# A graph sum by sorted scatter: all edges go through the scatter, against a kernel in which 48 columns of edges bypass it

## The chip, the cores and the metric

The kernel runs on one core of a Trainium2 chip. The metric is the device time of one execution in microseconds (us); the number given for a kernel is the median of its runs. The engines are named as in the profile: PE (TensorE, matmuls) with its weight loads PEld, DVE (VectorE), ACT (ScalarE), POOL (GpSimd, which issues the scatter), and SP (SyncE, which here only issues transfers).

## The reference

There are 6250 nodes with 128 features, and 206250 edges, each with a source node and 128 attributes, in no useful order of the source. Only the source is used:

```python
edge_aggr = jnp.zeros((n, HIDDEN)).at[row].add(edge_features)      # row = src: a sum of edge rows by node
combined = jnp.concatenate([x, edge_aggr, global_expand], axis=-1) @ W_c + b_c
h = softplus(combined @ W1 + b1)
h = softplus(h @ W2 + b2)
out = layernorm(x + h @ W3 + b3)
```

The sum over 206250 edges is the work; the small network behind it has 6250 rows.

## The kernel before, in words

**Columns and blocks.** Edge number p*1611 + c lies on partition p in column c, so the edges make 1612 columns of 128 (the last has 42). The nodes make 25 blocks of 256.

**Scatter and sum.** The columns are dealt to ten groups (`GROUPS`). For each group the kernel computes where every edge must go so that the edges of one block become neighbours in HBM, each block's stretch rounded up to whole units of 128, 256 or 512 rows (`positions`: DVE compares, scans and reductions, PE counts with matmuls of ones). `load_rows` brings a piece of ten columns of edge rows into SBUF (tile `rows`, SP queue), `code_rows` writes a number beside each row that names the node in its block and the group (line 597, on ACT), and `scatter_rows` sends the piece to HBM, one indirect transfer of 128 rows per column (line 605, POOL). One group later `reduce_steps` reads the sorted rows back: `load` brings 1024 rows (eight tiles of 128) into a tile `chunks` (SP queue); `match` makes a 0/1 matrix `hot` from the numbers, 256 wide per row (line 404, DVE, all eight tiles in one instruction); `total` multiplies the rows with it on PE (line 419) into the PSUM tile `part`, of which there are two, and DVE adds the result to the block's 256 columns of `sums_t` (line 424). A place in HBM is first filled with -1 (`fill_rows`), so that unused rows match nothing.

**The 48 columns.** The first 48 columns (`DIRECT`) are never scattered. `direct_steps` multiplies each column's 128 rows with a 0/1 matrix over all 6400 nodes, 512 at a time, so that every column meets 13 windows. ACT makes the matrix as relu(1 - |number - node|): one `Abs` per column and window (line 538) and one `Relu` per pair of columns (line 540), with three buffers `direct_hot`; PE multiplies two steps later (line 550) and DVE adds after twelve columns (line 554).

**Order.** PE, DVE, ACT and SP run a written order; all transfers of SP stand in one queue in the order of the program. For every piece of a group the program puts down: the load of the piece three ahead (`LEAD`), the code of the piece two ahead, the scatter of the piece, and then a share of the waiting steps: the positions of the next group, the sums of the group before, filling, and in groups 1 to 6 the 48 columns. The shares are set by `AHEAD`, so that a list is finished after 75% to 95% of the group's pieces. Each engine works through its own part of this order and never past an instruction that waits. After the last group its own sums are left, and then the network.

Of the kernel before, what the change touches and what calls it, by code (L numbers as in the profile page):

```python
# [7 lines left out]
F32 = mybir.dt.float32  # L8
# [35 lines left out]
def kernel(  # L44
# [33 lines left out]

    ND = min(DIRECT, T) // QUAD * QUAD
    c0 = ND  # L80
# [15 lines left out]

    iota_f = const.tile([P, WIDE], F32, name="iota_f")
    nc.gpsimd.iota(iota_f, pattern=[[1, WIDE]], base=0, channel_multiplier=0,
# [65 lines left out]
    with ExitStack() as phase:  # L164
        keep = phase.enter_context(tc.tile_pool(name="keep", bufs=1))
        per = phase.enter_context(tc.tile_pool(name="per", bufs=2))
        hots_p = phase.enter_context(tc.tile_pool(name="in_block", bufs=4))
        rows_p = phase.enter_context(tc.tile_pool(name="rows", bufs=LEAD + 2))
        chunks_p = phase.enter_context(tc.tile_pool(name="chunks", bufs=4))
        direct_p = phase.enter_context(tc.tile_pool(name="direct", bufs=1))  # L170
        hots = phase.enter_context(tc.tile_pool(name="hots", bufs=2))
# [3 lines left out]
        nc.vector.tensor_copy(iota_ps, iota_f[:, :BL])  # L175
# [7 lines left out]
        def whole_nodes(c0, c1):  # L183
# [10 lines left out]
            return part, node, wrap  # L194

        def node_codes(c0, c1):


            n = c1 - c0
            part, node, wrap = whole_nodes(c0, c1)  # L200
# [33 lines left out]
        def positions(g):  # L234
# [86 lines left out]
            def place(k, j0, j1):  # L321
                m = j1 - j0
                pr = by_col(ps.tile([P, 512], F32, name="pr", bufs=2))[:, :, :m]
# [45 lines left out]
            for k, (a, b) in enumerate(parts):  # L369
                for j0 in range(0, b - a, POS_COLS):  # L370
                    j1 = min(b - a, j0 + POS_COLS)
                    if j1 == b - a and k + 1 < len(parts):
                        steps.append(lambda k=k: scan(k + 1))
                    steps.append(lambda k=k, j0=j0, j1=j1: place(k, j0, j1))
                    todo.append(lambda k=k, j0=j0, j1=j1: place2(k, j0, j1))
                    if len(todo) > 1:
                        steps.append(todo.pop(0))
# [4 lines left out]
        def reduce_steps(g):  # L382
# [16 lines left out]
            def match(i):  # L399
# [3 lines left out]
                hot_of[i] = hot  # L403
                nc.vector.scalar_tensor_tensor(  # L404
# [25 lines left out]
            for i in range(n + 1):  # L430
                def one(i=i):
# [4 lines left out]
                    if i:  # L436
                        total(i - 1)
# [68 lines left out]
        def direct_steps():  # L506


            steps = []
            if not ND:  # L510
                return steps
            NW = -(-NB * BL // WIDE)
            less = keep.tile([P, NW, ND], F32, name="less")
            rows_in, hot_of, sum_of = {}, {}, {}

            def begin():

                first = keep.tile([P, NW], F32, name="first")
                nc.gpsimd.iota(first, pattern=[[WIDE, NW]], base=0, channel_multiplier=0,
                               allow_small_or_imprecise_dtypes=True)  # L520
                part, node, _ = whole_nodes(0, ND)
                nc.vector.tensor_copy(node, part)
                nc.vector.tensor_tensor(
                    less, node.unsqueeze(1).to_broadcast([P, NW, ND]),
                    first.unsqueeze(2).to_broadcast([P, NW, ND]), op=ALU.subtract)

            def load(c):
                n = min(SET, ND - c)
                rows_in[c] = direct_p.tile([P, SET, D], F32, name="direct_rows", bufs=2)
                sync_dma(rows_in[c][:, :n],  # L530
                         edge_attr[:P * T, :].rearrange("(p t) d -> p t d", p=P)[:, c:c + n, :])

            def compare(c, w, q):
                n = min(WIDE, NB * BL - w * WIDE)
                hot = direct_p.tile([P, QUAD, WIDE], F32, name="direct_hot", bufs=3)
                hot_of[c, w, q] = hot
                for j in range(QUAD):
                    nc.scalar.activation(hot[:, j, :n], iota_f[:, :n], AF.Abs,  # L538
                                         bias=less[:, w, c + q + j:c + q + j + 1], scale=-1.0)
                nc.scalar.activation(hot[:, :, :n], hot[:, :, :n], AF.Relu, bias=ones[:, :1],  # L540
                                     scale=-1.0)

            def add(c, w, q):
                n = min(WIDE, NB * BL - w * WIDE)
                k = min(SET, ND - c)
                hot = hot_of.pop((c, w, q))
                if q == 0:
                    sum_of[c, w] = ps.tile([P, WIDE], F32, name="direct_sum", bufs=1)
                for j in range(QUAD):
                    nc.tensor.matmul(sum_of[c, w][:, :n], rows_in[c][:, q + j, :], hot[:, j, :n],  # L550
                                     start=(q + j == 0), stop=(q + j == k - 1))
                if q + QUAD == k:
                    here = sums_t[:, w * WIDE:w * WIDE + n]
                    nc.vector.tensor_add(here, here, sum_of.pop((c, w))[:, :n])  # L554

            jobs = [(c, w, q) for c in range(0, ND, SET) for w in range(NW)
                    for q in range(0, min(SET, ND - c), QUAD)]
            steps += [begin, lambda: load(0)]
            for i in range(len(jobs) + 2):
                def one(i=i):  # L560
                    if i < len(jobs):
                        c, w, q = jobs[i]
                        if (w, q) == (NW // 2, 0) and c + SET < ND:
                            load(c + SET)
                        compare(*jobs[i])
                    if i > 1:
                        add(*jobs[i - 2])
                steps.append(one)
            return steps

# [42 lines left out]
        with tc.manual_schedule(engines={ET.PE, ET.DVE, ET.Activation, ET.SP}):  # L613
# [5 lines left out]
            put_dma(nc.scalar, src_i[:, ND:c1], by_part[:, ND:c1])  # L619
            put["todo"] = fill_rows(0)  # L620
            sync_dma(src_i[:, c1:T], by_part[:, c1:])
            if ND:
                sync_dma(src_i[:, :ND], by_part[:, :ND])
# [10 lines left out]
            node_codes(ND, c1)  # L634
# [11 lines left out]
            direct = direct_steps()  # L646


            left = [0.0] * G
            for g in range(1, G - 3):  # L650
                left[g] = max(0.0, groups[g][1] - groups[g][0]
                              - groups[g - 1][3] * groups[g - 1][2] / 3 - (26 if g == 3 else 0))
            direct_at = 0.0
            i = 0
            for g in range(G):
# [8 lines left out]
                for q in mine:  # L664
# [4 lines left out]

                    now = []  # L670
                    for w, todo in enumerate((prep, sums, other, filled)):
                        share = min(1.0, (q - mine[0] + 1) / (AHEAD[w] * len(mine)))
# [156 lines left out]
```

## Time and profile before

| what | value |
| --- | --- |
| time, median of 3 runs (lowest to highest) | 2886.88 us (2881.78 to 2890.8) |
| the profiled execution: its time, its span | 2886.88 us, 2884.8 us |
| first and last scatter start (line 605) | 25.7 us, 2674.6 us |
| scatters, busy, mean of one | 1564, 1497.8 us, 958 ns |
| last matmul of the sums starts (line 419) | 2779.7 us |
| busy: PE, DVE, ACT, POOL | 1931.5, 1376.6, 822.2, 1557.6 us |
| granted PE clock, mean | 0.836 |

The span runs from the first to the last instruction of one execution; the time holds 2.1 us more. A line of groups gives an operation's count, its busy time and the mean of one, and after the bar the time that its engine stood idle just before it, with what ended most of that. The releaser "issue" means that no wait shows in the profile, "remote" that a wait ended on a semaphore whose setter the profile does not tell. A row of windows gives, for a stretch of the span, the length, then busy time and count for each engine, the granted PE clock, the busy share of the DMA engines and GB/s.

### The profile page before, as it was taken

How to read it: one execution, taken by the hardware profiler on the slowest of the kernel's cores; microseconds unless marked ns; L12 is line 12 of the kernel's file. 1: busy time of each engine (PE TensorE's matmuls, PEld its weight loads, DVE VectorE, ACT ScalarE, POOL GpSimd, SP SyncE). 2: the span in 40 equal slices, each digit the busy share in tenths (PEclk: the TensorE clock that was granted, in tenths of full speed). 3: DMA queues.
4: the chain of work that ended last, by engine and by line, in shares of the span. 5: the costliest groups of instructions: out<-in, count | busy, mean ns of one | idle time of the engine just before them, and what ended most of it. 6: DMA issues, size and time to landing. Idle time of an engine off the chain costs nothing. (4 is left out here: it accounts for less than half of the span.)

```text
span 2884.8 us, 22170 instructions
## 1 busy us (share of the span) xinstructions
PE 1931.5 (67%) x6415; PEld 1254.3 (43%) x6415; DVE 1376.6 (48%) x1940; ACT 822.2 (29%) x1185; POOL 1557.6 (54%) x1635
## 2 busy tenths in 40 slices
PE   2267586677678748776667878567871677475874
PEld 0034244334445525454444645245551556354642
DVE  5255255334456316554234544244551665464965
ACT  0255454352233224243332334323320000000034
POOL 5746555566455565555665555655556356444025
PEclk9879698887889868898888888788996888687987
DMA  9688376554566535455534545344553456354421
GB/s 298 203 244 227 121 199 184 147 153 140 155 185 188 157 97 159 145 155 147 159 92 134 160 135 160 99 133 143 159 154 96 127 168 190 113 153 124 120 71 45
DMA packets 415375, 435.49 MB, mean 151 GB/s; under 512 B 37743, under 2 KB 305766, under 8 KB 415254
## 3 DMA queue, kind: packets, MB, share of 16 engines
q1 hardware_dynamic: 365062, 330.71, 40.7%
q0 software_dynamic: 50048, 103.35, 10.9%
q8 instruction: 51, 0.84, 0.1%
q14 instruction: 70, 0.57, 0.1%
q10 hardware_dynamic: 144, 0.02, 0.0%
HBM read 260.90 MB, written 173.03 MB: 150 GB/s over the span
## 5 line engine op out<-in xcount | busy, mean ns | idle before, releaser
L605 POOL DMA_INDIRECT place<-rows,pos x1564 | 1497.8, 958 | 1170.6 <-ACT rows L597 522.3
L419 PE MATMUL part<-hot,chunks 128*128 128x256 f32 x4472 | 1160.0, 415 | 446.1 <-DVE hot L404 274.2
L419 PEld LDWEIGHTS part<-hot,chunks 128*128 128x128 f32 x4472 | 916.0, 209 | 720.6 <-DVE hot L404 307.3
L424 DVE TENSOR_TENSOR sums_t<-sums_t,part 128x256 f32 x781 | 327.9, 420 | 1130.3 <-remote 676.2
L550 PE MATMUL direct_sum<-direct_hot,direct_rows 128*128 128x512 f32 (+1 forms) x1248 | 628.7, 637 | 267.4 <-DVE sums_t L554 137.5
L538 ACT ACTIVATE direct_hot<-iota_f,less 128x512 f32<-128x512 f32 (+1 forms) x624 | 405.0, 696 | 1351.6 <-remote 726.4
L404 DVE SCALAR_TENSOR_TENSOR hot<-chunks,iota_ps 128x2048 f32<-128x2048 f32 (+1 forms) x281 | 636.7, 2268 | 0.0
L550 PEld LDWEIGHTS direct_sum<-direct_hot,direct_rows 128*128 128x128 f32 x1248 | 251.8, 208 | 512.5 <-issue 397.7
L540 ACT ACTIVATE direct_hot<-direct_hot,ones 128x1024 f32<-128x1024 f32 (+1 forms) x312 | 348.1, 1116 | 10.1
L597 ACT COPY rows<-low 128x10 f32<-128x10 f32 (+1 forms) x159 | 30.4, 195 | 475.6 <-DMA place<-rows,pos 393.3
L554 DVE TENSOR_TENSOR sums_t<-sums_t,direct_sum 128x512 f32<-128x512 f32 (+1 forms) x52 | 34.6, 666 | 170.0 <-remote 85.7
L340 DVE TENSOR_REDUCE pos<-at 128x20 int32<-128x500 f32 (+2 forms) x80 | 87.1, 1089 | 2.7
L307 DVE TENSOR_TENSOR_SCAN so_far<-iota_ps,ib 128x1500 bf16<-128x1500 f32 (+5 forms) x29 | 85.7, 2954 | 0.0
L787 POOL TENSOR_TENSOR x_sb<-x_sb,b_all 128x512 f32<-128x512 f32 (+1 forms) x13 | 15.2, 1209 | 106.9 <-DMA x_sb<-in_x 106.9
L338 DVE TENSOR_TENSOR at<-pr,ib 128x500 f32<-128x500 f32 (+2 forms) x80 | 52.8, 660 | 21.2 <-remote 10.0
L716 ACT ACTIVATE away<-z_ps 128x512 f32<-128x512 f32 (+1 forms) x13 | 7.3, 561 | 191.4 <-DMA x_sb<-in_x 180.9
L775 POOL TENSOR_SCALAR y<-y,mv,rs 128x128 f32<-128x128 f32 (+1 forms) x49 | 38.1, 792 | 41.7 <-DVE rs L771 37.7
L324 PE MATMUL pr<-ib,upto_h 128*128 128x500 bf16 (+2 forms) x80 | 33.4, 418 | 39.1 <-DVE at L338 31.9
L325 PE MATMUL pr<-so_far,ones_h 128*128 128x500 bf16 (+2 forms) x80 | 33.5, 419 | 25.0 <-DVE last L310 23.1
L264 PE MATMUL small<-ib,ones_h 128*128 128x500 bf16 (+2 forms) x80 | 25.2, 427 | 29.4 <-DVE ib L253 29.4
L253 DVE TENSOR_TENSOR ib<-block,iota_ps 128x1500 bf16<-128x1500 bf16 (+5 forms) x29 | 44.3, 1551 | 0.0
L326 PE MATMUL pr<-more,ones_h 128*128 128x500 bf16 (+2 forms) x80 | 33.6, 419 | 3.5 <-issue 3.5
(115 smaller groups left out, 434.8 us busy)
## 6 DMA issues: line engine op xcount, KB each, us to landing
chunks<-place SPq DMA_DIRECT2D x278, 516.0 KB
rows<-in_edge_attr SPq DMA_DIRECT2D x155, 640.0 KB
place<-fill SPq DMA_DIRECT2D x252, 258.0 KB
place<-rows,pos POOLq DMA_INDIRECT x1564
x_sb<-in_x SPq DMA_DIRECT2D x24, 256.0 KB
direct_rows<-in_edge_attr SPq DMA_DIRECT2D x4, 768.0 KB
out<-y SPq DMA_DIRECT2D x12, 256.0 KB
chunks<-place SPq DMA_DIRECT2D x3, 258.0 KB
```

The costliest lines, as they stand in the source:

```text
L253: nc.vector.tensor_tensor(ib, block[:, a:b].unsqueeze(1).to_broadcast([P, NB, n]), iota_ps[:, :NB].unsqueeze(2).to_broadcast([P, NB, n]), ...
L307: nc.vector.tensor_tensor_scan(t, iota_ps[:, 1:2].to_broadcast([P, NB * n]), in_block[k][0], 0.0, op0=ALU.mult, op1=ALU.add)
L338: nc.vector.tensor_mul(at, got.pop((k, j0)), in_block[k][1][:, :, j0:j1])
L340: nc.vector.tensor_reduce(pos[:, a - c0 + j0:a - c0 + j1], at.rearrange("p b g -> p g b"), axis=mybir.AxisListType.X, op=ALU.add)
L404: nc.vector.scalar_tensor_tensor(hot[:, :m], chunks[i][:, :m, D:W].to_broadcast([P, m, BL]), float(1 + BL * g), iota_ps.unsqueeze(1).to_br ...
L419: nc.tensor.matmul(part[:, s - q, :], t[:, s * sub + j, :D], hot[:, s * sub + j], start=(j == 0), stop=(j == sub - 1))
L424: nc.vector.tensor_add(here, here, part[:, s - q, :])
L538: nc.scalar.activation(hot[:, j, :n], iota_f[:, :n], AF.Abs, bias=less[:, w, c + q + j:c + q + j + 1], scale=-1.0)
L540: nc.scalar.activation(hot[:, :, :n], hot[:, :, :n], AF.Relu, bias=ones[:, :1], scale=-1.0)
L550: nc.tensor.matmul(sum_of[c, w][:, :n], rows_in[c][:, q + j, :], hot[:, j, :n], start=(q + j == 0), stop=(q + j == k - 1))
L605: s = nc.gpsimd.indirect_dma_start(out=dst, out_offset=bass.IndirectOffsetOnAxis(ap=at, axis=0), in_=rows[:r, j, :], in_offset=None)
L775: nc.gpsimd.tensor_scalar(y[:r, q, :], y[:r, q, :], mv[:r, at + q, 0:1], rs[:r, 1, at + q:at + q + 1], op0=ALU.subtract, op1=ALU.mult)
```

## The change

All 1612 columns are scattered; `direct_steps`, its tiles and its PSUM bank are gone, and the node numbers are made in `node_codes` alone. Pieces have 20 columns, loaded two ahead (before: ten columns, three ahead). The groups are cut anew, with smaller ones at the end. The sums run two steps behind the comparison instead of one, with five `chunks` (four) and three `hot` (two). In the three last groups, `match` gives three of four loads to ACT (eight `Abs` of 256 and one `Relu` of 2048 per load). All step lists finish after 75% of a group's pieces. Three small tables `codes` are made on POOL at the start. `pr`, the PSUM tile of the positions, gets a third buffer; a filling transfer covers 768 rows instead of 512.

```diff
-LOAD_COLS = 10
+LOAD_COLS = 20
-GROUPS = ((40, 1), (120, 2), (200, 4), (240, 4), (240, 4), (240, 4), (212, 4), (140, 2), (88, 2),
-          (44, 1))
+GROUPS = ((40, 1), (120, 2), (210, 4), (240, 4), (240, 4), (240, 4), (200, 4), (126, 2), (84, 2), (56, 1),
+          (34, 1), (22, 1))
-DIRECT = 48
-SET = 12
-WIDE = 512
-QUAD = 2
-FILL = 4
+TAIL = 3
+FILL = 6
-AHEAD = (0.75, 0.95, 0.9, 0.75)
-LEAD = 3
+AHEAD = 0.75
+LEAD = 2
...
-        hots_p = phase.enter_context(tc.tile_pool(name="in_block", bufs=4))
+        hots_p = phase.enter_context(tc.tile_pool(name="in_block", bufs=5))
...
-        chunks_p = phase.enter_context(tc.tile_pool(name="chunks", bufs=4))
-        direct_p = phase.enter_context(tc.tile_pool(name="direct", bufs=1))
-        hots = phase.enter_context(tc.tile_pool(name="hots", bufs=2))
+        chunks_p = phase.enter_context(tc.tile_pool(name="chunks", bufs=5))
+        hots = phase.enter_context(tc.tile_pool(name="hots", bufs=3))
...
+        codes_of = {}
+        for g in range(max(0, G - TAIL), G):
+            codes_of[g] = keep.tile([P, BL], F32, name=f"codes{g}")
+            nc.gpsimd.iota(codes_of[g], pattern=[[1, BL]], base=1 + BL * g, channel_multiplier=0,
+                           allow_small_or_imprecise_dtypes=True)
...
+                if g in codes_of and i % 4 != 3:
+                    for j in range(m):
+                        nc.scalar.activation(hot[:, j], codes_of[g], AF.Abs,
+                                             bias=chunks[i][:, j, D:W], scale=-1.0)
+                    nc.scalar.activation(hot[:, :m], hot[:, :m], AF.Relu, bias=ones[:, :1],
+                                         scale=-1.0)
+                    return
...
-            for i in range(n + 1):
+            for i in range(n + 2):
                 def one(i=i):
                     if i + 2 < n:
                         load(i + 2)
                     if i < n:
                         match(i)
-                    if i:
-                        total(i - 1)
+                    if i > 1:
+                        total(i - 2)
...
-        def direct_steps():
...
-                    if left[g]:
-                        k = int(direct_at + 0.5)
-                        direct_at += len(direct) * left[g] / sum(left) / len(mine)
-                        now.append(direct[k:int(direct_at + 0.5)])
```

More of the change, by code (lines that the diff above doesn't have):

```diff
@@ L77 @@
     groups = []
-    ND = min(DIRECT, T) // QUAD * QUAD
-    c0 = ND
+    c0 = 0
     for size, sub in GROUPS:
@@ L94 @@
     dram = ctx.enter_context(tc.tile_pool(name="dram", bufs=1, space=bass.MemoryType.DRAM))
-    iota_f = const.tile([P, WIDE], F32, name="iota_f")
-    nc.gpsimd.iota(iota_f, pattern=[[1, WIDE]], base=0, channel_multiplier=0,
+    iota_f = const.tile([P, BL], F32, name="iota_f")
+    nc.gpsimd.iota(iota_f, pattern=[[1, BL]], base=0, channel_multiplier=0,
                    allow_small_or_imprecise_dtypes=True)
@@ L166 @@
         per = phase.enter_context(tc.tile_pool(name="per", bufs=2))
-        hots_p = phase.enter_context(tc.tile_pool(name="in_block", bufs=4))
+        hots_p = phase.enter_context(tc.tile_pool(name="in_block", bufs=5))
         rows_p = phase.enter_context(tc.tile_pool(name="rows", bufs=LEAD + 2))
-        chunks_p = phase.enter_context(tc.tile_pool(name="chunks", bufs=4))
-        direct_p = phase.enter_context(tc.tile_pool(name="direct", bufs=1))
-        hots = phase.enter_context(tc.tile_pool(name="hots", bufs=2))
+        chunks_p = phase.enter_context(tc.tile_pool(name="chunks", bufs=5))
+        hots = phase.enter_context(tc.tile_pool(name="hots", bufs=3))
         ps = phase.enter_context(tc.tile_pool(name="ps", bufs=1, space=PSUM))
         iota_ps = ps.tile([P, BL], F32, name="iota_ps")
-        nc.vector.tensor_copy(iota_ps, iota_f[:, :BL])
+        nc.vector.tensor_copy(iota_ps, iota_f)
         src_i = keep.tile([P, TC], I32, name="src_i")
@@ L181, with node_codes @@
         fill = keep.tile([P, FILL * W], F32, name="fill")
-        def whole_nodes(c0, c1):
+        codes_of = {}
[3 more added lines that the diff above has]
+                           allow_small_or_imprecise_dtypes=True)
+        def node_codes(c0, c1):
             n = c1 - c0
@@ L193, in whole_nodes @@
             nc.vector.tensor_add(part, node, wrap)
[L194 to L200, printed above, removed]
             part_i = wrap.bitcast(I32)
@@ L322, in place @@
                 m = j1 - j0
-                pr = by_col(ps.tile([P, 512], F32, name="pr", bufs=2))[:, :, :m]
+                pr = by_col(ps.tile([P, 512], F32, name="pr", bufs=3))[:, :, :m]
                 nc.tensor.matmul(pr, upto_h, in_block[k][1][:, :, j0:j1], start=True, stop=False)
@@ L375, in positions @@
                     todo.append(lambda k=k, j0=j0, j1=j1: place2(k, j0, j1))
-                    if len(todo) > 1:
+                    if len(todo) > 2:
                         steps.append(todo.pop(0))
@@ L504, in node_rows @@
             return steps
-        def direct_steps():
[L509 to L569, printed above, removed]
@@ L618 @@
             by_part = src[:P * T].rearrange("(p t) -> p t", p=P)
-            put_dma(nc.scalar, src_i[:, ND:c1], by_part[:, ND:c1])
+            put_dma(nc.scalar, src_i[:, :c1], by_part[:, :c1])
             put["todo"] = fill_rows(0)
             sync_dma(src_i[:, c1:T], by_part[:, c1:])
-            if ND:
-                sync_dma(src_i[:, :ND], by_part[:, :ND])
             if R:
@@ L633 @@
                 put["todo"].pop(0)()
-            node_codes(ND, c1)
+            node_codes(0, c1)
             for i in range(LEAD - 1):
@@ L644 @@
             sync_dma(b3_row, b3.rearrange("(o d) -> o d", o=1))
[L646 to L653, printed above, removed]
             i = 0
@@ L668 @@
                     i += 1
+                    share = min(1.0, (q - mine[0] + 1) / (AHEAD * len(mine)))
                     now = []
                     for w, todo in enumerate((prep, sums, other, filled)):
-                        share = min(1.0, (q - mine[0] + 1) / (AHEAD[w] * len(mine)))
                         upto = int(round(len(todo) * share))
```

## The prediction

> **What bounds the kernel now.** I read the groups first, because no engine is busy for the whole span.
>
> ```profile
> L605 POOL DMA_INDIRECT place<-rows,pos x1564 | 1497.8, 958 | 1170.6 <-ACT rows L597 522.3
> L419 PE MATMUL part<-hot,chunks 128*128 128x256 f32 x4472 | 1160.0, 415 | 446.1 <-DVE hot L404 274.2
> ...
> L550 PE MATMUL direct_sum<-direct_hot,direct_rows 128*128 128x512 f32 (+1 forms) x1248 | 628.7, 637 | 267.4 <-DVE sums_t L554 137.5
> ```
>
> The scatters follow each other from 25.7 to 2675.5 us, so POOL's busy time and idle time together set nine tenths of the span. Behind the scatter lie 104.6 us of sums and 104.7 us of network. Next come the waits (total us, times, longest), to split POOL's idle time.
>
> ```profile
> ACT direct_hot L538 <- remote: 726.4, 63, 24.8
> DVE sums_t L424 <- remote: 676.2, 70, 33.4
> POOL place L605 <- ACT rows L597: 522.3, 69, 17.0
> POOL place L605 <- issue: 454.3, 1462, 2.6
> ...
> POOL place L605 <- DMA rows<-in_edge_attr: 101.8, 7, 32.9
> ```
>
> "Issue" is the step from scatter to scatter, 454.3 / 1462 = 0.31 us each; with the 0.958 us of one a column costs 1.268 us. The 1564 cost 1983.2 of 2649.8 us, and 666.6 us are true waits. Most end on the code copy at line 597, which stands on ACT's queue behind the comparisons of the 48 columns (lines 538, 540), and these wait for PE to free a buffer. So far it looks as if ACT were the brake. The third view, windows around 2175 us (PE, PEld, DVE, ACT, POOL, clock, DMA), and the timeline show something else.
>
> ```profile
> 2175.00:2205.00 30.00, 0.82 (x4) 0.38 (x2) 0.00 (x0) 0.62 (x3) 22.68 (x25) 0.59 0.17 56
> 2205.00:2232.00 27.00, 0.00 (x0) 0.00 (x0) 0.84 (x2) 0.42 (x2) 15.19 (x16) 0.50 0.19 61
> ```
>
> ```profile
> 2169.62 3.62 PE L419 MATMUL part<-hot,chunks 128*128 128x256 f32 x16
> ...
> 2205.75 0.36 SPq L141 DMA_DIRECT2D chunks<-place  x1
> 2205.76 0.87 DVE L424 TENSOR_TENSOR sums_t<-sums_t,part 128x256 f32 x2 [35.74 <-issue]
> ```
>
> PE has finished the product at 2173.24 us, yet DVE, which waits for it, and SP, which waits for a free buffer, go on 32.5 us later, at the same moment. In between only POOL works, with one scatter after another from 2161.9 to 2224.8 us. The 63 and 70 "remote" waits are of this kind: what PE reports is heard late during a long row of scatters, and POOL and the sums take turns. Whether that is a law of the chip no row says, but the price can be read where ACT compares nothing, in the last stage (windows of line 605, then of line 419; count in brackets).
>
> ```profile
> 2257.60:2675.50 417.90, 212.45 (x222) 0.81 0.51 147
> 2355.00:2421.10 66.10, 38.27 (x40) 0.90 0.62 185
> 2587.00:2675.50 88.50, 42.06 (x44) 0.77 0.44 127
> ```
>
> ```profile
> 2257.60:2675.50 417.90, 260.49 (x998) 207.34 (x997) 0.81 0.51 147
> 2355.00:2421.10 66.10, 55.71 (x224) 45.56 (x223) 0.90 0.62 185
> 2587.00:2675.50 88.50, 52.55 (x195) 40.83 (x194) 0.77 0.44 127
> 2675.50:2780.10 104.60, 86.33 (x339) 63.84 (x337) 0.95 0.35 94
> ```
>
> A load of eight tiles is 16 matmuls. From 2257.6 to 2675.5 us POOL waited 417.9 - 222 x 1.268 = 136.4 us while 62.4 loads were summed: 2.19 us per load. The best stretch gives (66.1 - 50.7) / 14 = 1.10, the last (88.5 - 55.8) / 12.2 = 2.68. This is the stage most like the changed kernel: scatter and sums alone.
>
> **The change part by part.** *Scatters.* 48 more on POOL: 48 x 1.268 = +60.9 us, all on the path. 1612 x 1.268 = 2044.0 us.
>
> *The 48 columns on ACT and PE.* Gone are 405.0 + 348.1 us of ACT, 628.7 us of PE and 34.6 us of DVE (line 554). None of it is path by itself; what goes is the copy's wait of 522.3 us. What is late next is the row load: SP's queue holds it behind loads of sorted rows, and these wait for PE's report. So I do not book 522.3 us, but replace all waits by the price per load. The groups before the last hold 64 + 168 + 308 + 3 x 336 + 296 + 174 + 132 + 80 + 58 = 2288 tiles (units by the formula for `nsc`, times 1, 2 or 4), or 286 loads. As now, some of the last but one's stay over: 339 - 136 of its 272 matmuls, 75%, which here is 5.4 loads. The other 280.6 x 2.19 = 614.5 us, against 666.6 now: -52.1 us. Bounds: 1.10 and 2.68 per load.
>
> *Pieces of 20, loaded two ahead; sums two steps behind; one more buffer of each kind.* A piece is 25.4 us of scatter, and POOL can hold 40 columns, 50.7 us. That lets rows of scatters grow; no stage of before has this form throughout. The second step and the buffers let DVE compare while it would have waited, but `part` still has two buffers, so PE is two loads ahead at most. One helps, one hurts, by amounts that only the bounds above hold; I take zero and keep the bounds.
>
> *Last groups.* After the scatter 339 / 16 = 21.2 loads took 104.6 us, 4.94 each. Now 46 tiles (5.75 loads) and the 5.4 left over: 11.2 x 4.94 = 55.3 us, -49.3 us. ACT's part of the comparisons: `Abs` on 256 took 492 ns, `Relu` 721 ns on 512 and 1148 on 1024, so about 2.0 us on 2048; a load costs ACT 8 x 0.492 + 2.0 = 5.9 us where DVE took 2.28. Three in four are 17.8 us per four loads, 4.4 each, under the 4.94 measured; if the first are late, all eleven cost 5.9, 66 us. I keep 55.3. But ACT's queue now holds code copies behind comparisons again: in the written order line 597 for the last group's three pieces stands behind six, two and three such loads, 11 x 5.9 = 65 us, with 34 + 20 + 1 columns of scatter, 69.7 us, to cover them. The cover just holds; if loads come late it is gone, and a wait of 0 to 40 us (seven loads) stands on the path. I take zero.
>
> *Cover and small things.* The filling (168 transfers for 252) and the three tables on POOL lie before the first scatter or beside it, and that scatter waits for positions until 25.7 us; if the tables came late they cost one or two us. The positions keep their cost; a third `pr` buffer frees PE, not DVE.
>
> A rule against this change: The Trainium skill, "TensorE: Matmul & The Clock Gate", "What's actually happening", says that PE falls to half rate after an idle window of about 3.4 us and needs as long a busy one to come back. This trace agrees (clock 0.50 in the idle window above), and with 628.7 us of matmuls taken out PE will be idle more often. By the rule alone each of before's 76 waits of POOL for copies and rows would cost 1.7 us of lost rate, an estimate of 130 us if all of it showed, and the sum would be 2976 us. The 2.19 us were measured at clock 0.81, with such restarts in them, so nothing is added.
>
> **Sum.** 25.7 + 2044.0 + 614.5 + 55.3 + 104.7 = 2844.2 us of span, and 2.1 outside it: 2846 us. The profiled execution is the median run, 2886.88, so this is 41 us or 1.4% less. It turns to no change at 614.5 + 41 = 655.5 us of waits, 2.34 us per load.
>
> **The rivals.** *Slower: longer rows of scatters.* With ACT's stops gone, POOL runs its 40 columns through, PE's report stays unheard for them, and the waits come back on the row loads. For it: the row of 40 scatters from 2421.1 to 2471.3 us, after which DVE still waits until 2476.8 us, and the last window. At 2.68 us per load, +137: 2983 us; at the mean since 2161.9 us, (513.6 - 272 x 1.268) / (1108 / 16) = 2.44, +70: 2916 us. It decides from 2.34 on. Against it: 1.10 in a stretch with full work on POOL.
> *Much faster: ACT was the brake.* The first six groups need 193.5 loads for 1250 columns, a thinner mix than the 62.4 for 222; if they wait only 1.10 each, -211: 2635 us. Against it: 676.2 us of DVE's waits do not name ACT.
> *No gain in the tail.* The late codes of the last pieces, +40: 2886 us.
>
> **How the numbers follow.** The measurement can tell about 0.3%, 2878.2 to 2895.5. My case has 0.40, of which 0.33 lies below and 0.05 within that; the faster rival 0.17; the slower one 0.35, with 0.02 within; the tail 0.08, dealt 0.02, 0.03, 0.03. Faster 0.52, same 0.10, slower 0.38. The range: below, to 1.63 us per load, 2690; above, to the 2.68 of the last window, 2983, rounded to 2990. My case's own range is 1.9 to 2.4 per load, 2765 to 2905.
>
> **What would show it.** 1612 scatters of 0.958 us with 0.31 between; no waits for the copy before the three last groups, and row loads named in their place; "remote" waits of DVE still there; 550 to 680 us of waits in all; about 55 us from the last scatter to the network. Wrong, if POOL's waits in the first six groups are under 250 us (the brake was ACT) or over 550 (rows of 40 scatters and more).

## The result and the profile after

The changed kernel takes 3129.58 us (median of 4 runs, 3115.77 to 3141.65) against 2888.84 us (4 runs, 2881.78 to 2895.21) for the kernel before beside it: ratio 1.083, interval [1.077, 1.090], so 241 us slower. The forecast was 2846 us, faster than before. The profiled execution is the longest but one of the four, 3139.8 us with a span of 3137.6 us.

One thing is needed to read the numbers below. The experiments ran in five sessions on four chips, and in two of them the kernel before took 2197 and 2201 us, in the other three 2839 to 2858 us; chip 4 was seen in both conditions. The session of the result is of the long kind, like the trace that the forecast was made from. I call the two kinds "on time" and "late", after what the traces show below, and every ratio is against the kernel before in the same session. The changed kernel with nothing altered ran in late sessions alone. A ratio leaves out executions over 1.5% above the fastest of their kernel, which takes three of the seven executions of the kernel before out of the last session.

The groups of after, as counterpart to the first lines shown of before (busy, mean of one, then idle time just before them):

```profile
L542 POOL DMA_INDIRECT place<-rows,pos x1612 | 1548.1, 960 | 1425.9 <-issue 482.2 <-DMA rows<-in_edge_attr 196.1 <-DVE sums_t L426 188.9
L421 PE MATMUL part<-hot,chunks 128*128 128x256 f32 x4668 | 1253.0, 429 | 1056.7 <-DVE sums_t L426 563.0 <-issue 426.4 <-DVE hot L406 65.8
L426 DVE TENSOR_TENSOR sums_t<-sums_t,part 128x256 f32 x888 | 372.5, 419 | 1551.3 <-remote 1201.2 <-issue 219.1 <-PE part L421 101.3
```

One scatter costs what it did, and 482.2 / 1569 = 0.31 us lies between two. But POOL's idle time has grown, although the code copy that ended most of it before is no longer named. The waits (total us, times, longest) say what took its place:

```profile
DVE sums_t L426 <- remote: 1201.2, 78, 50.4
...
POOL place L542 <- issue: 482.2, 1569, 1.9
...
POOL place L542 <- DMA rows<-in_edge_attr: 196.1, 10, 37.0
POOL place L542 <- DVE sums_t L426: 188.9, 8, 43.4
POOL place L542 <- DVE hot L406: 185.8, 6, 52.2
...
POOL place L542 <- DVE pos L334: 114.9, 3, 71.8
...
POOL place L542 <- ACT rows L534: 30.9, 3, 16.8
```

DVE's remote waits are the first thing to see: 676.2 us before, 1201.2 now, the longest 50.4 us instead of 33.4. POOL now waits seldom and long: for row loads, for sums and comparisons on DVE, for positions. Windows of the scatter (line 542), then of the sums' matmuls (line 421), for the first six groups, the rest, and the sums after the last scatter:

```profile
85.80:2251.00 2165.20, 1200.15 (x1251) 0.70 0.49 149
2251.00:2981.60 730.60, 309.08 (x322) 0.75 0.40 119
```

```profile
85.80:2251.00 2165.20, 824.29 (x3064) 654.64 (x3064) 0.70 0.49 149
2251.00:2981.60 730.60, 380.39 (x1420) 298.88 (x1420) 0.75 0.40 119
2981.60:3036.40 54.80, 48.33 (x184) 31.25 (x184) 1.00 0.30 78
```

In the first six groups POOL waits 2165.2 - 1251 x 1.268 = 578.9 us for 3064 / 16 = 191.5 loads, 3.02 us per load; in the rest 730.6 - 322 x 1.268 = 322.3 us for 88.75 loads, 3.63 us. The clock is 0.70 and 0.75. In the forecast's terms the span is 28.2 (start) + 2044.0 (scatters) + 909.4 (waits) + 54.8 (sums after the last) + 101.2 (network) = 3137.6 us. All terms but one lie within 4 us of the forecast; the waits are 909.4 instead of 614.5 (before: 666.6).

The timeline of after around 700 us shows how one such wait comes about (start, length, engine, instruction; in brackets the idle time before). The scatters run without a stop from 595.7 to 735.7 us:

```profile
659.66 3.83 PE L421 MATMUL part<-hot,chunks 128*128 128x256 f32 x17
...
675.16 0.58 PE L421 MATMUL part<-hot,chunks 128*128 128x256 f32 x1 [1.52 <-issue]
...
685.66 0.10 PEld L258 LDWEIGHTS <-ones_h 128*128 128x128 bf16 x1 [2.70 <-issue]
687.06 0.57 PE L258 MATMUL small<-ib,ones_h 128*128 128x500 bf16 x1 [2.21 <-issue]
688.46 0.10 PEld L258 LDWEIGHTS <-ones_h 128*128 128x128 bf16 x1 [2.69 <-issue]
689.86 0.57 PE L258 MATMUL small<-ib,ones_h 128*128 128x500 bf16 x1 [2.23 <-issue]
...
719.29 0.37 SPq L135 DMA_DIRECT2D chunks<-place  x1
719.30 0.88 DVE L426 TENSOR_TENSOR sums_t<-sums_t,part 128x256 f32 x2 [50.40 <-remote]
...
734.76 0.96 POOL L542 DMA_INDIRECT place<-rows,pos  x1 [0.30 <-issue]
...
750.82 0.87 SPq L135 DMA_DIRECT2D chunks<-place  x2
750.83 0.88 DVE L426 TENSOR_TENSOR sums_t<-sums_t,part 128x256 f32 x2 [26.83 <-remote]
```

At 659.7 us PE does 17 matmuls in 3.83 us. By 685 us it begins one instruction, weight load or matmul, in 1.40 us, with nothing but "issue" ahead of it. The last matmul for `part` here has ended by 675.7 us (ends of matmuls are modelled), yet the addition on DVE that waits for PE, and SP's load that waits for a free buffer, go on at 719.3 us, in the same moment; the trace's event of the semaphore that both wait for stands at 719.27 us. So in a long row of scatters PE's reports are late, and PE itself falls to a crawl. This report came while POOL was still scattering, as did the one at 2205.75 us in the trace of before: a stop is not the only thing that lets one out.

The table sorts the 888 products of one profiled execution of the changed kernel in a late session (e13) by the time since the row of scatters began in which DVE was otherwise ready to add: how many additions came over 1 us late, and by how much on the mean. It is worked out from the trace, from each product's last matmul, DVE's instruction before the addition, and the start of the row (a row ends where POOL stops for over 1.5 us).

| in the row since | additions | over 1 us late | mean delay, all |
| --- | --- | --- | --- |
| 0 to 8 us | 159 | 2 | 0.1 us |
| 8 to 12 us | 61 | 16 | 1.7 us |
| 12 to 20 us | 55 | 27 | 8.4 us |
| 20 to 36 us | 29 | 13 | 6.6 us |
| 36 us and more | 53 | 26 | 11.7 us |
| POOL stopped | 531 | 27 | 0.2 us |

For some 8 us, six or seven scatters, hardly anything happens; then the delays set in. Of the 70 additions that came over 5 us late, 44 went on while the same row was still running. The same count over e9 below, the changed kernel with pieces of 10 on time, has 713 additions at 36 us and more into a row, and none over 5 us late: long rows cost only in the late condition.

### The profile page after: what moved, and what is told of

Its sections match the earlier page's. It is cut to its first block, busy times and chain, and to the rows that moved or that the text cites. A ratio compares the mean times of both kernels' runs of the same rounds, so it can differ in the third digit from the quotient of the medians.

```text
span 3137.6 us, 18723 instructions
## 1 busy us (share of the span) xinstructions
PE 1460.6 (47%) x5389; PEld 1075.6 (34%) x5389; DVE 1384.4 (44%) x2049; ACT 178.2 (6%) x344; POOL 1608.6 (51%) x1685
## 5 line engine op out<-in xcount | busy, mean ns | idle before, releaser
L542 POOL DMA_INDIRECT place<-rows,pos x1612 | 1548.1, 960 | 1425.9 <-issue 482.2
L421 PE MATMUL part<-hot,chunks 128*128 128x256 f32 x4668 | 1253.0, 429 | 1056.7 <-DVE sums_t L426 563.0
L421 PEld LDWEIGHTS part<-hot,chunks 128*128 128x128 f32 x4668 | 984.8, 216 | 1313.4 <-DVE sums_t L426 624.5
L426 DVE TENSOR_TENSOR sums_t<-sums_t,part 128x256 f32 x888 | 372.5, 419 | 1551.3 <-remote 1201.2
L406 DVE SCALAR_TENSOR_TENSOR hot<-chunks,iota_ps 128x2048 f32<-128x2048 f32 x275 | 621.8, 2263 | 34.4 <-DMA chunks<-place 34.4
L534 ACT COPY rows<-low 128x20 f32<-128x20 f32 (+3 forms) x85 | 18.7, 223 | 2758.9 <-DMA place<-rows,pos 2367.4
L301 DVE TENSOR_TENSOR_SCAN so_far<-iota_ps,ib 128x1500 bf16<-128x1500 f32 (+8 forms) x31 | 88.5, 2856 | 0.0
L401 ACT ACTIVATE hot<-codes,chunks 128x256 f32<-128x256 f32 x150 | 61.8, 494 | 149.5 <-remote 118.5
L489 PE MATMUL small<-ident,x_sb 128*128 128x128 f32 (+1 forms) x49 | 10.3, 344 | 99.3 <-DMA x_sb<-in_x 55.4
L247 DVE TENSOR_TENSOR ib<-block,iota_ps 128x1500 bf16<-128x1500 bf16 (+8 forms) x31 | 46.0, 1498 | 0.0
```

The source lines that it names most:

```text
L247: nc.vector.tensor_tensor(ib, block[:, a:b].unsqueeze(1).to_broadcast([P, NB, n]), iota_ps[:, :NB].unsqueeze(2).to_broadcast([P, NB, n]), ...
L301: nc.vector.tensor_tensor_scan(t, iota_ps[:, 1:2].to_broadcast([P, NB * n]), in_block[k][0], 0.0, op0=ALU.mult, op1=ALU.add)
L401: nc.scalar.activation(hot[:, j], codes_of[g], AF.Abs, bias=chunks[i][:, j, D:W], scale=-1.0)
L406: nc.vector.scalar_tensor_tensor(hot[:, :m], chunks[i][:, :m, D:W].to_broadcast([P, m, BL]), float(1 + BL * g), iota_ps.unsqueeze(1).to_br ...
L421: nc.tensor.matmul(part[:, s - q, :], t[:, s * sub + j, :D], hot[:, s * sub + j], start=(j == 0), stop=(j == sub - 1))
L426: nc.vector.tensor_add(here, here, part[:, s - q, :])
```

## The experiments

Theory A says that the rows of scatters decide: where they are long, PE's reports come late, sums and loads stand still, and POOL then waits for its row loads. Rival B says that the pieces of 20 and the new order cost by themselves; rival C that ACT's comparisons were a brake; rival D that a row load of 20 columns is too large. In the expectations of the first four runs theory A is called R, "theory T" puts the loss on the new last groups, and the "theory A" of e4 is what is rival C here.

**First session (on time; kernel before 2196.65 us, 2194.22 to 2199.24).** e1 makes shorter pieces, three ahead as in the kernel before:

```diff
-LOAD_COLS = 20
+LOAD_COLS = 10
...
-LEAD = 2
+LEAD = 3
```

> The changed kernel with pieces of 10 columns loaded three ahead, as before, all else as changed. Theory R (rows of scatters: while POOL scatters without a stop for more than about ten us, what PE reports is heard only after the stop, so every longer row costs more): POOL can now hold 30 columns instead of 40 to 60, its stops come sooner and are shorter; POOL's waits in the first seven groups fall from 578 us to 480 to 540, time 3030 to 3090. Theory T (the new cuts of the last groups and ScalarE's comparisons cost it all): nothing changes but noise, 3100 to 3150.

Measured: 2252.08 us (2246.49 to 2256.62), ratio 1.0244 [1.0225, 1.0264].

e2 takes the last groups back to sizes like those of before, and all comparisons back to DVE:

```diff
-GROUPS = ((40, 1), (120, 2), (210, 4), (240, 4), (240, 4), (240, 4), (200, 4), (126, 2), (84, 2), (56, 1),
-          (34, 1), (22, 1))
+GROUPS = ((40, 1), (120, 2), (224, 4), (240, 4), (240, 4), (240, 4), (236, 4), (140, 2), (88, 2),
+          (44, 1))
...
-TAIL = 3
+TAIL = 0
```

> The changed kernel with the ends of the groups cut as before (140, 88 and 44 columns at the end, the 48 columns spread over two earlier groups) and all comparisons on VectorE. Theory R: only the tail changes; its waits of 322 us for 322 columns become about those of before, 169 us for 272, the sums after the last scatter get 50 us longer again; time 3000 to 3070, still well over before. Theory T: the whole excess goes, time 2900 to 2950, which is before plus 48 scatters.

Measured: 2256.49 us (2255.49 to 2257.48), ratio 1.0271 [1.0254, 1.0288].

e3 puts a small fill on POOL after every scatter of the changed kernel, ordered between it and the next:

```diff
+        pause = keep.tile([P, 128], F32, name="pause")
...
+                    w = nc.gpsimd.memset(pause, 0.0).ins
+                    tc.add_manual_dep(w, s.ins.name, NO_SYNC, reason="one order on POOL")
```

> The changed kernel with a memset of 128 x 128 on GpSimd after every scatter, which stretches the step from 1.27 to about 1.45 us, so that scatters alone take about 2340 us. Theory R in its form that the rate matters: the reports are heard again in a row, VectorE's waits on nothing named fall from 1201 us to under 400, POOL's waits from 909 to under 400, time 2650 to 2900. Theory R in its form that only a full stop counts: the waits stay, time 3250 to 3400. Theory T: waits stay in the tail, and the slower step adds up to 290 us: 3250 to 3420.

Measured: 2379.18 us (2377.28 to 2379.68), ratio 1.0829 [1.0810, 1.0847]. The step from scatter to scatter went from 1.263 to 1.350 us.

e4 is the kernel before with all columns scattered:

```diff
-GROUPS = ((40, 1), (120, 2), (200, 4), (240, 4), (240, 4), (240, 4), (212, 4), (140, 2), (88, 2),
+GROUPS = ((40, 1), (120, 2), (224, 4), (240, 4), (240, 4), (240, 4), (236, 4), (140, 2), (88, 2),
...
-DIRECT = 48
+DIRECT = 0
```

> The kernel before with no columns kept from the scatter (the 48 go into two groups, all 1612 are scattered), all else as before. Theory R: ScalarE no longer stops POOL early, rows get longer than the 25 us of now, VectorE's waits on nothing named rise from 762 us; with 61 us for 48 scatters time is 2950 to 3060. Theory A (ScalarE's comparisons were what held POOL, and the rest of the change is what made it slow): the 522 us of waits on the copies go, time 2550 to 2800.

Measured: 2257.27 us (2253.33 to 2259.72), ratio 1.0271 [1.0253, 1.0289].

The waits of e4 show a different machine:

```profile
POOL place L605 <- issue: 464.1, 1522, 0.3
...
DVE sums_t L424 <- PE part L419: 206.0, 151, 6.1
...
POOL place L605 <- DMA rows<-in_edge_attr: 10.6, 2, 10.3
```

There is no remote wait of DVE, and POOL runs from 26.3 to 2071.6 us practically without a stop. Then the price of the 48 columns stands alone: 48 x 1.263 = 60.6 us, and 2257.27 - 2196.65 = 60.6 us. The variants without the 48 columns are alike (2252 to 2257 us), with either size of piece: B, by which pieces and order cost wherever the kernel runs, falls. The shorter last groups earn next to nothing here. In e1 the sums after the last scatter end 53.6 us behind it, in e2 79.8 us; but POOL's waits in e1 are 30.7 us, in e2 0.9 us (at 1.268 us a column; the two also differ in the size of piece). The stops come back before the small groups. e3 only measured its own fills, since nothing was late. All four expectations were written for the late condition, so none of their numbers was tested here; whether an even, slower pace as in e3 would help when reports are late was not run.

**Second session (late; kernel before 2857.64 us, 2835.33 to 2866.7).** e5 is the changed kernel again. e6 has pieces of 10 in it, still two ahead:

```diff
-LOAD_COLS = 20
+LOAD_COLS = 10
```

e7 is the kernel before with 24 compared columns; e8 has 72 in the same way, and 188 for the 236:

```diff
-GROUPS = ((40, 1), (120, 2), (200, 4), (240, 4), (240, 4), (240, 4), (212, 4), (140, 2), (88, 2),
+GROUPS = ((40, 1), (120, 2), (200, 4), (240, 4), (240, 4), (240, 4), (236, 4), (140, 2), (88, 2),
...
-DIRECT = 48
+DIRECT = 24
```

> The changed kernel as it is. Its sum, without POOL's waits: 48 scatters at 1.263 us are +60.6 us, and its shorter last groups gave -53 us from the last scatter to the end in the first comparison. Theory A (the +240 us came from long rows of scatters in which PE's reports are heard late, and only where they are late): where the kernel before takes about 2197 us the changed one takes 2197 + 60.6 - 0 to 53 = 2205 to 2258 us, and where it takes about 2888 us the changed one takes about 3130 us again. Rival B (the pieces of 20 and the order of the steps cost time by themselves, on any chip): some 2350 us or more where the kernel before takes 2197, that is a ratio near 1.08 in both places.

> The changed kernel with pieces of 10 columns, loaded two ahead (20 columns held on POOL's side in place of 40). Theory A: where reports are late, rows of scatters can hold at most 20 columns, 25 us, waits fall to before's 2.2 us per load or less, and the time to 2850 to 2950 us against 3130; where reports are on time, 25 us of cover are enough for loads of 9 to 17 us, and the time is the changed kernel's within 15 us. Rival B (20 columns are too few to cover a row load): slower than the changed kernel by over 30 us where reports are on time.

> The kernel before with 24 columns compared by ACT and 1588 scattered, in place of 48 and 1564. Theory A, where reports are on time (kernel before 2197 us): the price is the scatter alone, 24 x 1.263 = +30.3 us, 2227 us. Where reports are late (2888 us): half of ACT's stops go, so rows of scatters grow and the time rises by more than 30 us, up to 150 us. Rival C (ACT's comparisons are a brake): half of it goes, so 24 x 1.263 less half of the copy's wait of 522 us, some 230 us faster where that wait is there.

> The kernel before with 72 columns compared by ACT and 1540 scattered. If POOL's scatters are the bound and ACT and PE have room, 24 x 1.263 = -30.3 us: 2166 us where the kernel before takes 2197. If PE becomes the bound (314 us more of matmuls on some 1900 us of busy time in 2197 us of span) or ACT (some 375 us more on 822), slower than the kernel before, up to 2300 us. Where reports are late (2888 us), theory A gives no more than -30 us, since ACT's stops already break the rows; rival C (ACT the brake) gives 100 to 250 us more.

Measured: e5 3121.44 us (3102.36 to 3135.88), 1.0951 [1.0887, 1.1016]; e6 2902.33 us (2883.48 to 2916.93), 1.0184 [1.0123, 1.0245]; e7 2891.48 us (2881.6 to 2913.8), 1.0155 [1.0087, 1.0223]; e8 2949.86 us (2946.45 to 2988.22), 1.0378 [1.0289, 1.0466]. So one constant, the size of a piece, is worth 219 us here; in the first session versions with 10 and with 20 took the same time. e7 costs 34 us where its scatters alone are 30: half of the comparisons are gone, and nothing is gained. Rival C, which gave 230 us, falls. e8 went against both: theory A gave a gain of no more than 30 us here and rival C 100 to 250 more, and with 24 scatters fewer it took 92 us more. Its waits put that on the copy behind the comparisons:

```profile
POOL place L605 <- ACT rows L597: 640.6, 82, 20.2
...
DVE sums_t L424 <- remote: 503.1, 49, 48.2
```

The remote waits are lower than before's 676.2 us, but POOL now waits 640.6 us for the copy (522.3 in the trace of before), while PE is busy for 72% of the span.

**Third session (on time; kernel before 2201.46 us, 2197.78 to 2204.95).** e9 has pieces of 10 loaded four ahead in the changed kernel:

```diff
-LOAD_COLS = 20
+LOAD_COLS = 10
...
-LEAD = 2
+LEAD = 4
```

e10 puts a pause on POOL behind every ten scatters of the changed kernel, and the next ten behind the pause:

```diff
+        pause = keep.tile([P, 512], F32, name="pause")
...
+                hold["row"].append(s.ins)
+                if len(hold["row"]) == 10:
+                    for _ in range(8):
+                        w = nc.gpsimd.memset(pause, 0.0).ins
...
```

e11 is the kernel before with two pieces ahead, and e12 the kernel before with pieces of 5, still three ahead:

```diff
-LEAD = 3
+LEAD = 2
```

```diff
-LOAD_COLS = 10
+LOAD_COLS = 5
```

> The changed kernel with pieces of 10 columns loaded four ahead: again 40 columns held, but in small loads. Theory A (the length of the rows of scatters decides): where reports are late it takes the changed kernel's time, 3050 to 3150 us, not the 2902 us of pieces of 10 loaded two ahead. Rival D (the size of one row load decides: a load of 20 columns takes the transfer engines from the other traffic): about 2900 us. Where reports are on time: 2250 us by both, as pieces of 10 loaded three ahead gave.

> The changed kernel with a pause on POOL after every tenth scatter: eight fills of 512 columns of a tile that nobody reads, some 0.54 us each by the 221 ns for 128 columns and 5421 ns for 6400, 4.3 us in all, 161 times: 694 us of extra work on POOL. Theory A: where reports are late they now come in every pause, so DVE's remote waits fall from 1200 us to under 500 and most of the 909 us of waits goes: 28 + 2044 + 694 + 51 + 105 = 2922 us plus what waits are left, 2900 to 3100 us, no slower than without the pauses. Rivals B and D (rows of scatters don't matter): the pauses come on top for the most part, 3500 us or more. Where reports are on time: 2200 + 694 = 2890 us at least.

> The kernel before with its pieces of 10 loaded two ahead in place of three: at most 20 columns in a row. A version that might beat both. Theory A: where reports are late, slightly faster, 0 to 60 us under the kernel before, since its rows of scatters are mostly of 20 columns already. Where reports are on time: unchanged within 10 us. Rival B (less cover for the row loads costs): slower by 20 us or more.

> The kernel before with pieces of 5 columns loaded three ahead: 15 columns, 19 us, in place of 30. Theory A: where reports are late, rows of scatters are shorter and the time falls by 30 to 150 us; the limit is a row load of 9 to 17 us, which 19 us of scatter just cover. Where reports are on time: 0 to 60 us slower, from loads that are not covered. Rival B: slower in both.

Measured: e9 2255.31 us, 1.0250 [1.0229, 1.0271]; e10 2946.16 us, 1.3379 [1.3356, 1.3403]; e11 2200.04 us, 0.9992 [0.9982, 1.0002]; e12 2195.18 us, 0.9967 [0.9956, 0.9979]. On time the pauses, 680 us of fills, cost 691 us against e9, which has pieces of 10: they are paid in full. The question was left open, and e9, e10 and e12 ran again.

**Fourth session (late; kernel before 2838.94 us, 2822.11 to 2853.15).** e13 is the changed kernel, e14 is e9, e15 is e10, e16 is e12.

> The changed kernel as it is, beside the others of this call. Where PE's reports are late (kernel before about 2860 us): 3100 to 3140 us. Where they are on time (kernel before about 2200 us): theory A says 2200 + 60.6 - 0 to 15 = 2245 to 2260 us, as the two versions of it with pieces of 10 gave (2252 and 2255 us); rival B says the pieces of 20 cost there too, 2280 us or more.

> Pieces of 10 loaded four ahead in the changed kernel: 40 columns held, in small loads. Theory A (length of the rows): where reports are late 3050 to 3150 us. Rival D (size of one load): about 2900 us there. Where they are on time, 2255 us by both.

> The changed kernel with a pause of 4.3 us on POOL after every tenth scatter. Where reports are on time the 161 pauses cost 691 us, all of them on the path (2946 us on one chip). Theory A: where reports are late they come in the pauses, and the time is again 2946 us or little more, up to 3050, so less than the 3121 us without pauses although POOL has 691 us more to do. Rivals B and D: 3500 us or more.

> The kernel before with pieces of 5 loaded three ahead, 15 columns held. Where reports are on time 0.3% faster than the kernel before, as measured on one chip (ratio 0.9967). Theory A: where they are late, 30 to 150 us faster than the kernel before; rivals B and D: no faster, or slower.

Measured: e13 3113.6 us (3095.78 to 3127.62), 1.0959 [1.0881, 1.1036]; e14 2925.88 us (2917.84 to 2928.93), 1.0300 [1.0243, 1.0358]; e15 2959.15 us (2955.0 to 2960.01), 1.0428 [1.0372, 1.0484]; e16 2735.73 us (2721.61 to 2743.3), 0.9649 [0.9595, 0.9703].

The same kernel in both conditions is the cleanest view of what "late" is. The waits of e9, on time:

```profile
POOL place L542 <- issue: 464.2, 1521, 0.7
...
DVE sums_t L426 <- PE part L421: 119.4, 134, 5.1
...
PE part L421 <- issue: 0.2, 1, 0.2
```

And of e14, late:

```profile
DVE sums_t L426 <- remote: 1061.2, 81, 44.6
POOL place L542 <- issue: 497.4, 1537, 10.9
POOL place L542 <- DMA rows<-in_edge_attr: 450.0, 36, 27.7
...
PE part L421 <- issue: 402.5, 60, 38.1
```

Nothing in the program differs, and PE's own issue time goes from 0.2 to 402.5 us with DVE's remote waits.

e14 missed theory A's expectation (3050 to 3150 us) and met rival D's. The groups of e15 decide between them; its pieces are of 20 columns, as in e13:

```profile
L544 POOL DMA_INDIRECT place<-rows,pos x1612 | 1545.1, 959 | 502.1 <-issue 478.1 <-DMA w_sb<-in_L_gnn_W 22.0 <-DVE sums_t L428 0.5
L555 POOL MEMSET pause<- 128x512 f32 x1288 | 678.3, 527 | 65.0
```

Apart from issue and 22 us at the start POOL waits for nothing any more. DVE's remote waits in e15:

```profile
DVE sums_t L428 <- remote: 70.8, 33, 4.6
```

From 1174.1 us (e13) to 70.8, with the row loads of 20 columns untouched, and 154 us faster although POOL has 678 us of fills more to do. B and D, for which the pauses would have come on top (3500 us or more), fall. What e14 really tested is seen in the rows as they ran. In e13 1232 of the 1612 columns ran in rows of 30 and more (counted at stops of over 1 us), in e14 904, in e6 850, in e15 none. With pieces of 10 most rows end after 10 or 20 columns, with two pieces ahead as with four; it is the row as it runs that counts, not the number of columns allowed. That the lead would set it was the error in my expectation. Rows as they ran are counted afterwards and are themselves an outcome; the runs that set their length are e15 and, below, e17. e16 tests the same from the kernel before: its columns in rows of 30 and more are 305 (400 in the trace of before), its remote waits 518.0 us (676.2; that trace is of another session), and it is 103 us faster than the kernel before beside it.

**Fifth session (late; kernel before 2841.06 us, 2806.14 to 2868.77).** e17 halves e15's pause, e18 is e4.

```diff
-                    for _ in range(8):
+                    for _ in range(4):
```

> The changed kernel with a pause of 2.1 us (four fills) on POOL after every tenth scatter. Where reports are on time: 2255 + 161 x 2.1 = 2600 us. Where they are late, if 2.1 us of stop are enough for a report: 28 + 2044 + 346 + 60 of waits left + 51 + 105 = 2634 us, faster than the kernel before (about 2840). If a report needs its 3.4 us after the last scatter: few are heard in such a pause, the remote waits of DVE stay over 700 us, and the time is 2850 to 3150 us.

> The kernel before with all its 1612 columns scattered and no column compared by ACT; pieces of 10 loaded three ahead, the order and the last groups of before. Where reports are late: if the 48 columns cost only their scatters, 2840 + 61 = 2900 us (24 of them cost 34 us), and the pieces of 20 are the larger part of the change's 270 us; if ACT's stops were what broke the rows, 3050 us or more. Where they are on time, 2257 us as measured.

Measured: e17 2605.44 us (2603.87 to 2611.31), 0.9215 [0.9135, 0.9294]; e18 2909.84 us (2889.46 to 2932.26), 1.0296 [1.0168, 1.0424]. Half the pause is enough, as the groups and waits of e17 show:

```profile
L544 POOL DMA_INDIRECT place<-rows,pos x1612 | 1549.7, 961 | 519.3 <-issue 467.7 <-DMA w_sb<-in_L_gnn_W 21.7 <-ACT hot L403 18.4
L555 POOL MEMSET pause<- 128x512 f32 x644 | 341.4, 530 | 27.8
```

```profile
DVE sums_t L428 <- remote: 66.6, 31, 5.2
```

369 us of pauses replace 889 to 909 us of waits. Whether a stop of 2 us lets the reports out, or a row of 10 is merely too short for them to pile up, these two runs do not part: both have rows of 10. Nor do they part the break from the slower pace on the mean, 1.50 us a column in e17 and 1.72 in e15, against 1.27 within a row. And e18 gives the first part of the change by itself:

```profile
DVE sums_t L424 <- remote: 1097.3, 96, 40.3
...
POOL place L605 <- DMA rows<-in_edge_attr: 520.4, 54, 22.2
```

The copy's wait is gone but for 6 us, as the change wants, and the row loads have taken its place; POOL's waits are 2671.8 - 2044.0 = 627.8 us, against 666.6 in the trace of before, which is of a session 46 us slower.

**The sum of it, in late sessions.** Scattering the 48 columns costs some 84 us by e18's ratio, with an interval from 48 to 120. The pieces of 20 cost 188 us (e13 less e14) or 219 us (e5 less e6). The rest of the change, e14 against e18, cannot be told from nothing: ratios 1.0300 and 1.0296, within some 40 us either way. Together 272 to 303 us, for 264 and 275 measured (e5, e13).

**A version that beats both.** e16 (e12), the kernel before with `LOAD_COLS = 5`, is faster than both kernels late (0.9649 against the kernel before) and equal to the kernel before within 0.5% on time (0.9967 [0.9956, 0.9979]), where versions of the changed kernel took 2252 to 2257 us. e17 is much faster late, but by e10 its pauses would be paid in full on time; there it wasn't run.

## Why the prediction was wrong

*The 48 scatters* (+60.9 us): right, 60.6 us on time. Late, scattering them costs some 84 us (48 to 120), since the waits change with it.

*The copy's waits go, the row loads' come* (-52.1 us net): right in kind, but there was no gain in it. In e18's own session the cost of 84 us (48 to 120) less 60.9 for the scatters leaves the waits 23 us longer, with an interval from -13 to +59. The price per load was too low. Worked out in the same way, e18 gives 627.8 / (4232 / 16) = 2.37 us per load, e14 679.5 / (4444 / 16) = 2.45. At 2.37 to 2.45 instead of 2.19 the waits of 280.6 loads would have been 665 to 687 us, 50 to 73 more, and the sum 2897 to 2919 us: already past the turning point of 2.34.

*Pieces of 20, loaded two ahead: zero.* This is the step that failed. I wrote that they let rows of scatters grow, that the additional buffers help, and booked the two against each other without a price, with bounds of 1.10 and 2.68 us per load. I also took 40 columns, what POOL can hold, for the longest row; loads that land while POOL scatters made rows of 100 and 120. The changed kernel pays 909.4 / (4484 / 16) = 3.24, outside the bounds. Against e14's 2.45 that is 0.8 us per load, some 220 us, the size of nearly the whole loss. The bounds came from stretches of a kernel whose rows of scatters were mostly of 10 and 20 columns and at most of 50; no stretch of it could show rows of 60 to 120. A bound taken from the trace holds only while the thing that sets the price stays within what the trace shows.

*The tail* (-49.3 us): right as booked. From the last scatter to the network 54.8 us, forecast 55.3. But the term was drawn too narrowly: ahead of the last four groups and the last column POOL stops 19, 32, 72, 54 and 17 us, 194 us in all, ended by a row load, a load of sorted rows, the positions (line 334, 71.8 us), ACT's comparisons (line 401) and the code copy, where I had put 0 to 40 us on the code copy. The copy took 30.9 us in all. On time the same was seen small, 26 us gained after the last scatter and 30 lost ahead of it (e1, e2).

*The rivals.* "Slower: longer rows of scatters" is what happened, by its own mechanism, and its sign of it came true: waits over 550 us in the first six groups (578.9). Its price, 2.44 to 2.68 per load, was undersized for the reason above. "ACT was the brake" is refuted by e7 and e18: with fewer comparisons, or none, nothing was gained.

*The clock.* The granted clock fell, 0.836 to 0.73, and the mean matmul for `part` rose from 415 to 429 ns. The Trainium skill, "TensorE: Matmul & The Clock Gate", "What's actually happening", says that PE drops to half rate after an idle window of some 3.4 us. The fall agrees, but a low clock is not what makes POOL wait: e10 and e15 ran at 0.739 and 0.741 and in both the waits for PE's work were gone, and e4 at 0.82 costs exactly its scatters. The estimate of 130 us by that rule would have moved the sum in the right direction for the wrong reason.

*The chances.* 0.38 for slower was too little, and the range ended at 2990 us because it ended with the bounds of the failed step. The trace spoke for the rival in the one row of 40 scatters that I named and set aside.

## What to carry to other kernels

Where an engine stops often, ask what its stops are good for before taking them away: here rows of ten scatters mostly ended before PE's reports fell behind, and longer pieces turned many short waits into fewer long ones. An edit that changes how long an engine runs without a stop wants a price of its own, and if no stretch of the trace is of that kind, the bounds must reach past the worst stretch. And compare a kernel only with runs of the same session: the same program took 2200 and 2840 us on one chip.

## What was not expected of the hardware

Two conditions 29% apart, 2201 and 2841 us for the kernel before on chip 4. They aren't of the program (e9 and e14 are the same) and not of one chip; what sets them stays open.

In the late condition not only reports are late: PE itself issues one instruction in 1.40 us where it had done a weight load and a matmul in 0.23. That looks like reports leaving through a path that drains slowly while POOL scatters, until it is full and holds PE back; this is argued from the timeline and not shown. That PE is held back by something else, and its reports with it, would look the same.

A pause of 2.29 us in 14.9 us was enough to take DVE's remote waits from 1174.1 us (e13) to 66.6 us (e17, another late session). An idle engine would have looked like the thing to remove.
